# A feed-forward block split by batch element, one half in the tail of the attention before it, one beside the first group of the attention after it, and a fixed VectorE order for the first tokens

## The chip, the cores and the metric

The kernel runs as one program on one core of a Trainium2 chip. A time is the device time of one execution in microseconds (us). The engines are TensorE (PE, matmuls and transposes; PEld is its weight load), VectorE (DVE), ScalarE (ACT), GpSimd (POOL) and the DMA queue of SyncE (SP). All arithmetic is in 32-bit floats.

## What is computed

A batch of B = 2 sequences of 512 tokens of width 512 goes through eight residual blocks. The change touches the first three:

```
x = x + attn_latent(layernorm(x))   # 32 heads, 12-wide query latents, 4-wide key latents
x = x + ffn_lora(layernorm(x))      # y = x @ W.T + bias, plus per batch element a low-rank
                                    # adapter x @ A.T @ B.T, chosen by lora_start_indices
x = x + attn_gqa(layernorm(x))      # 32 query heads in 8 groups of 4, causal, rotary
...                                 # ffn_lora, attn_mla, ffn_moe, attn_mha, ffn_moe
layernorm(x) = (x - mean) / sqrt(var + 1e-5)
```

## The kernel before

x stays in on-chip memory as eight tiles of 128 tokens (x0 to x3 are batch element 0, x4 to x7 are 1). A layer norm of a tile is `centred` (L170: statistics on VectorE, a power on GpSimd in `inv_sqrt`, then xn on VectorE, in one of two "xn" buffers) and `place` (L184: four transposes on PE, one copy on ScalarE into xT of the batch element). Products against x read xT. PSUM has eight banks, handed out in turn (`turn`, L145); before `hold` (L150) each turn takes a tile from a pool, after it one of eight fixed tiles.

Most engines' instruction order is chosen by the framework's scheduler, which may move an instruction ahead of others when it is ready by its own reckoning. Inside `tc.manual_schedule(engines={...})` the named engines keep the order of the program. An instruction on an engine's queue waits in order: what stands behind a waiting one waits too.

**First attention** (`attn_latent_small`, L399). `prepare(b)` makes the layer norms of four tiles, key latents, query latents, the queries of all heads and the values. `prepare(0)` runs first, in the scheduler's order; the eleven pieces of `prepare(1)`, `fold` and `fold_bias` are handed to `run_quartets` as `extra`. There are 16 quartets u (batch element, half, index) of four heads. For a quartet: `score` (16 matmuls with 32 rows each, for the maxima, each reduced on VectorE), `maxima`, `transposed` (16 matmuls with 32 rows, each followed by an exponential on ScalarE into a probabilities tile of one of three kinds), `values`. In step u of the loop (L343) the scores of u+1 alternate with the transposed scores of u; then come values(u) and maxima(u+1). Pieces `divide`, `flatten`, `project` and `norms` of the quartet before lie between; after quartet 7 and 15 they finish a batch element: divide by the sums, flatten on GpSimd, project on PE and add to x. `norms` (L629) makes the feed-forward block's layer norms of x0 to x3 during quartets 8 to 10. PE keeps the program's order here. In the last two steps only transposed scores and values of quartet 15 are left, then its divide, flatten and project.

**Feed-forward block** (`ffn_lora`, L665). Loads the weight (1 MB, buffer kind "w8", five buffers) and the adapter, scales the adapter by `k.coef` (from `adapter_coefficients`, L644), and makes one adapted weight for each batch element: eight 48-row matmul pairs, each added to the weight on VectorE. Then, for each of eight tiles, a `chain` of four matmul steps (eight instructions in the trace), the sum into x, and a layer norm: beside batch 0's products those of x4 to x7 for this block, beside batch 1's products those of x0 to x3 for the next attention (`back=True`, a permuted token order).

**Second attention** (`attn_gqa`, L707). Loads wdk, rotary tables, the first group's weights; `latents(0, m)` are four chains on xT of batch 0. A group of four heads m then goes through query products (`queries`, three parts per pair of heads; sums of weights on GpSimd, additions and rotation on VectorE and GpSimd), `softmax` per head, and `beside(m, j)`, which places the work of neighbouring groups after head j: prepare_keys(m+1) at j = 2, prepare_values(m+1) at j = 3, values(m-1), output(m-1, ...). For m = 0 there is no earlier group. PE keeps the program's order here too.

Of the kernel before, what the change touches and what calls it, by code (L numbers as in the profile page):

```python
# [45 lines left out]
class Block:  # L46


    def __init__(self, ctx, tc, x, out):
        nc = self.nc = tc.nc  # L50
        self.tc = tc
        self.out = out
        pool = lambda name, bufs, **kw: ctx.enter_context(tc.tile_pool(name=name, bufs=bufs, **kw))
        self.const = pool("const", 1)
        self.w = pool("w", 2)
        self.work = pool("work", 2)
        self.small = pool("small", 6)
# [19 lines left out]
        self.warm()  # L77
# [5 lines left out]
    def warm(self):  # L83


        ps = self.tr()
        for i in range(56):
            self.nc.tensor.transpose(ps[:, bass.ts(i % 4, P)], self.ident, self.ident)

    def load_x(self, b):  # L90
# [76 lines left out]
        return last.ins  # L167


    def centred(self, t, bias=None):  # L170

        nc = self.nc
        stats = self.sm(6, "ln_stats")
        nc.vector.bn_stats(stats, self.x[t])
        mv = self.sm(2, "ln_mv")
        nc.vector.bn_aggr(mv, stats)
        rstd = self.inv_sqrt(mv[:, 1:2], 1.0, 1e-5)
        xn = self.work.tile([P, D], F32, tag="xn", name="xn")
        nc.vector.tensor_scalar(xn, self.x[t], mv[:, 0:1], rstd, ALU.subtract, ALU.mult)
        if bias is not None:  # L180
            self.add_bias(t, bias)
        return xn
# [27 lines left out]
        self.nc.gpsimd.tensor_tensor(self.x[t], self.x[t], bias, ALU.add)  # L210

    def add_to_x(self, t, ps):
        self.nc.vector.tensor_tensor(self.x[t], ps, self.x[t], ALU.add)

# [119 lines left out]
                )  # L334

    @staticmethod
    def run_quartets(n, score, maxima, transposed, values, after, extra=()):

        due, extra = [], list(extra)
        for u in range(-1, n + 1):  # L343
            pieces = [due.pop(0)] if due else []
            for j in range(NT):
                for m, (kind, g) in enumerate(
                    ((0, 0), (1, 1), (0, 2), (1, 3), (0, 1), (1, 0), (0, 3), (1, 2))
                    if j
                    else ((0, 0), (0, 1), (0, 2), (0, 3), (1, 0), (1, 1), (1, 2), (1, 3))
                ):  # L350
                    if kind == 0 and u + 1 < n:
                        score(u + 1, j, g)
                    if kind == 1 and 0 <= u < n:
                        transposed(u, j, g)
                if extra and u >= 0:
                    extra.pop(0)()
                elif pieces and j < 3:
                    of, done = pieces[0]
                    if done < len(after):
                        after[done](of)  # L360
                        pieces[0] = (of, done + 1)
            for of, done in pieces:
                for f in after[done:]:
                    f(of)
            if 0 <= u < n:
                values(u)
                due.append((u, 0))
            if u + 1 < n:
                maxima(u + 1)

    @staticmethod
    def run_ordered(n, lead, order, score, maxima, transposed, values, after):
# [26 lines left out]
def attn_latent_small(k, a):  # L399
# [7 lines left out]
    nc, tc = k.nc, k.tc  # L407
    with ExitStack() as ctx:
# [19 lines left out]
        for i in range(2):  # L428
            m = one([P, NT, P], f"nm{i}")
# [7 lines left out]
        for vk in vals:  # L437
            nc.gpsimd.memset(vk, 0.0)
        halves = one([P, 8], "halves")
        nc.vector.tensor_scalar(halves, bqk, 0.5, None, ALU.mult)  # L440

        def prepare(b):

# [28 lines left out]
            def values():  # L472

                tp = k.turn()
                for t in range(NT):
                    nc.tensor.transpose(tp[:, bass.ts(t, P)], keys[b][:, bass.ts(t, P)], k.ident)
                part = tp.rearrange("p (t d) -> p t d", t=NT)[:, :, 0:5]
                for i in range(4):
                    nc.vector.tensor_copy(vals[b][:, :, i, 5 * i : 5 * i + 5], part)

            norms = [lambda t=t: k.layernorm(b * NT + t, k.turn) for t in range(NT)]
            return norms + [latents, queries, lambda: heads(0), lambda: heads(1), values]

        def fold():

# [22 lines left out]
                k.add_bias(t, bias)  # L508

        folded = one([P, D], "folded")  # L510
        for piece in prepare(0):
            piece()
        k.masks()
        adapter_coefficients(k, a)
        extra = prepare(1) + [fold, fold_bias]

        quartets = [(b, half, i) for b in range(B) for half in range(2) for i in range(4)]
        qm, probs, sums, ctxs = {}, {}, {}, {}
# [26 lines left out]
        def transposed(u, kc, g):  # L545
            b, half, i = quartets[u]
            if (u, kc) not in probs:
                n = (4 * u + kc) % 3
                if n == 0:
                    probs[u, kc] = k.other()  # L550
                else:
                    pool, tag, bufs = ((lp, "pT", 2), (k.w, "w8", 5))[n - 1]
                    probs[u, kc] = pool.tile([P, 4, S], F32, tag=tag, name="pt", bufs=bufs)
# [75 lines left out]
        def norms(u):  # L629

            i = u - len(quartets) // 2 + 1
            if i in (1, 2):
                for t in (2 * i - 2, 2 * i - 1):
                    k.place(t, normal.pop(t), k.turn)
            if i in (0, 1):
                for t in (2 * i, 2 * i + 1):
                    normal[t] = k.centred(t)

        after = [divide, flatten, project, norms]
        with tc.manual_schedule(engines={mybir.EngineType.PE}):  # L640
            k.run_quartets(len(quartets), score, maxima, transposed, values, after, extra)


def adapter_coefficients(k, a):  # L644
# [17 lines left out]
    nc.vector.tensor_reduce(k.coef, r, AX.X, ALU.add)  # L662


def ffn_lora(k, a):  # L665

    nc, tc = k.nc, k.tc  # L670
    R = 48
    with ExitStack() as ctx:
        lp = ctx.enter_context(tc.tile_pool(name="f0", bufs=2))
        w = k.load(a["f0_w"], [P, KC, D], "w8", 5)

        la = k.load(a["f0_a"], [P, D], "w3", 6)
        lb = k.load(a["f0_b"], [P, D], "w3", 6)
        bias = k.load_row(a["f0_bias"], D, "bias")
        nc.vector.tensor_scalar(la, la, k.coef, None, ALU.mult)

        adapted = [k.w.tile([P, KC, D], F32, tag="w8", name="adapted", bufs=5) for b in range(B)]
        for m in range(KC):
            out = [k.turn() for b in range(B)]
            for b in range(B):
                own = slice(64 * b, 64 * b + R)
                nc.tensor.matmul(
                    out[b], la[own, bass.ts(m, P)], lb[own], start=True, stop=True
                )
            for b in range(B):
                nc.vector.tensor_tensor(adapted[b][:, m], out[b], w[:, m], ALU.add)  # L690

        for t in range(NT):
            k.add_bias(t, bias)
        for b in range(B):
            for t in range(NT):
                ps = k.turn()
                k.chain(
                    ps, [(k.xT[b][:, c, bass.ts(t, P)], adapted[b][:, c]) for c in range(KC)]
                )
                k.add_to_x(b * NT + t, ps)  # L700
                if b == 0:
                    k.layernorm(NT + t, k.turn, bias=bias)
                else:
                    k.layernorm(t, k.turn, back=True)


def attn_gqa(k, a, bound):  # L707

# [8 lines left out]
    with ExitStack() as ctx:  # L717
# [188 lines left out]
        def beside(m, j):  # L906


            before = m - 1 if 0 < m <= len(groups) else None

            normal(m, j, 5, 1, True)
# [877 lines left out]
```

## Time and profile before

| | |
|---|---|
| Three runs | 2122.04, 2124.99, 2126.02 us; median 2124.99 |
| The profiled execution | 2125.91 us, of which its span is 2124.2 us |
| Busy share of PE, DVE, ACT, POOL | 96%, 64%, 35%, 46% |
| Mean granted TensorE clock | 0.982 of full |
| First scores on PE | 29.45 us |
| Last scores of the first attention end | 277.2 us |
| First chain of the feed-forward block | 306.1 us |
| First latents of the second attention | 338.86 us |
| First exponents of its group 0 | 369.43 us |

The profile is one execution of the program, with every engine's instructions in time. In the rows that the prediction shows, "sc<-qm,keys" means that tile sc was written from qm and keys; "x8" counts instructions; a bracket gives the idle time just before on that engine and what ended it. L164 is `chain`, L190 and L195 the transposes and the copy of `place`, L524 the score matmul, L555 and L558 the transposed score and its exponential, L566 the values, L588 to L624 divide, flatten and project, L686 and L690 the adapter matmul and its addition, L829 to L874 the queries and their rotation, L237 the second attention's scores, L309 its values. Matmuls overlap in the pipeline, so a row's duration is longer than its spacing to the next.

### The profile page before, as it was taken

To read this page: it belongs to the slowest core of one execution; us is meant where nothing else is said; L and a number is where in the kernel's file an instruction comes from. 1 tells how busy PE (TensorE), PEld (TensorE's weight loads), DVE (VectorE), ACT (ScalarE), POOL (GpSimd) and SP (SyncE) were. 2 spreads that over 40 slices of the span, in tenths; PEclk is the share of its full clock that TensorE was granted. 3 is DMA by queue.
4 is the path that set the end of the run, shared out by engine and by line. 5 is a ranking of instruction groups with operands and counts; after the bars stand their busy time and mean duration, and the time that the engine had idled before them with its cause. 6 is when DMAs were issued, how large, how long until landed. Compare 5 with 4: busy or idle time off the path is not lost. (4 is left out here: it accounts for less than half of the span.)

```text
span 2124.2 us, 40108 instructions
## 1 busy us (share of the span) xinstructions
PE 2046.3 (96%) x15556; PEld 1154.9 (54%) x15556; DVE 1349.7 (64%) x3575; ACT 744.9 (35%) x2072; POOL 967.1 (46%) x1239
## 2 busy tenths in 40 slices
PE   8999999899999999999999988999999989999998
PEld 5444435666666666666666444545454444554654
DVE  6578754765675566666765547666666684855845
ACT  2465631222222222222322135454445311441531
POOL 1101013767565467666763246555555556115220
PEclk8999999999999999999999989999999999999999
DMA  3000022222222222222221321010101003002001
GB/s 99 16 1 1 21 90 76 83 71 70 90 73 72 82 73 80 71 90 71 73 71 36 115 60 50 25 50 25 50 22 50 3 6 68 3 2 40 2 2 40
DMA packets 70220, 107.43 MB, mean 51 GB/s; under 512 B 13698, under 2 KB 50690, under 8 KB 63236
## 3 DMA queue, kind: packets, MB, share of 16 engines
q1 hardware_dynamic: 69380, 103.71, 15.7%
q8 instruction: 126, 2.06, 0.4%
q10 hardware_dynamic: 640, 1.05, 0.3%
q14 instruction: 74, 0.61, 0.1%
HBM read 80.61 MB, written 2.10 MB: 39 GB/s over the span
## 5 line engine op out<-in xcount | busy, mean ns | idle before, releaser
L258 ACT ACTIVATE room<-room,nmax 128x128 f32<-128x128 f32 (+3 forms) x384 | 212.1, 554 | 475.6 <-DVE nmax L248 474.4
L269 POOL TENSOR_SCALAR room<-room,invs 128x128 f32<-128x128 f32 (+3 forms) x384 | 197.8, 536 | 138.6 <-DVE invs L266 138.6
L309 PE MATMUL sc<-turned,vals 32*128 32x128 f32 (+7 forms) x1090 | 188.2, 421 | 0.0
L309 PE MATMUL tp<-turned,vals 32*128 32x384 f32 (+7 forms) x720 | 163.8, 410 | 2.5 <-DVE q L838 1.9
L237 PE MATMUL sc<-kT,q 128*32 128x256 f32 (+3 forms) x1496 | 135.4, 397 | 11.4 <-DVE invs L266 7.9
L282 DVE STREAM_TRANSPOSE turned<-room 128x1152 f32<-128x1152 f32 x80 | 109.0, 1363 | 41.2 <-POOL room L269 38.7
L309 PEld LDWEIGHTS sc<-turned,vals 32*128 32x128 f32 (+1 forms) x1090 | 121.8, 170 | 9.2 <-issue 3.3
L309 PE MATMUL pj<-turned,vals 32*128 32x256 f32 (+7 forms) x602 | 124.8, 421 | 1.3 <-DVE turned L282 1.3
L205 POOL TENSOR_TENSOR rstd<-ve,mhalf 128x1 f32<-128x1 f32 x80 | 44.5, 560 | 166.7 <-DVE ve L203 142.6
L873 POOL TENSOR_TENSOR q<-q,cosq 128x512 f32<-128x512 f32 x60 | 89.4, 1491 | 60.6 <-DVE t L870 60.6
L237 PE MATMUL tp<-kT,q 128*32 128x32 f32 (+15 forms) x1072 | 98.5, 401 | 11.1 <-DVE invs L266 7.3
L309 PEld LDWEIGHTS tp<-turned,vals 32*128 32x128 f32 (+1 forms) x720 | 96.6, 168 | 15.6 <-issue 8.3
L237 PE MATMUL pj<-kT,q 128*32 128x96 f32 (+15 forms) x1048 | 100.0, 415 | 1.7 <-DVE invs L266 0.9
L164 PE MATMUL sc<-w,room 128*128 128x512 f32 (+1 forms) x224 | 100.1, 593 | 0.0
L309 PE MATMUL av<-turned,vals 32*128 32x384 f32 (+7 forms) x372 | 99.9, 419 | 0.0
L269 POOL TENSOR_SCALAR probs<-probs,invs 128x128 f32<-128x128 f32 (+3 forms) x128 | 65.8, 534 | 64.4 <-DVE invs L266 60.5
L164 PE MATMUL sc<-w,ctxT 128*128 128x512 f32 x208 | 94.1, 595 | 0.0
L258 ACT ACTIVATE probs<-probs,nmax 128x128 f32<-128x128 f32 (+3 forms) x128 | 71.1, 556 | 65.3 <-DVE nmax L248 64.0
L874 POOL TENSOR_TENSOR q<-q,t 128x512 f32<-128x512 f32 x64 | 88.3, 1380 | 7.2 <-DVE q L873 3.2
L1135 POOL TENSOR_TENSOR t<-t,sinq 128x512 f32<-128x512 f32 x32 | 40.9, 1278 | 110.9 <-DVE invs L266 102.3
L281 DVE STREAM_TRANSPOSE turned<-room 128x128 f32<-128x128 f32 x80 | 24.4, 305 | 99.4 <-POOL room L269 99.3
L555 PE MATMUL sc<-qm,keys 32*128 32x512 f32 x198 | 85.5, 637 | 0.0
(610 smaller groups left out, 6284.0 us busy)
## 6 DMA issues: line engine op xcount, KB each, us to landing
w<-in_b_wq SPq DMA_DIRECT2D x16, 1024.0 KB, 5.0
w<-in_b_wo SPq DMA_DIRECT2D x16, 1024.0 KB, 5.7
vals<-v SPq DMA_DIRECT2D x256, 64.0 KB, 2.0
w<-in_m_wo SPq DMA_DIRECT2D x8, 1024.0 KB, 5.8
w<-in_b_wk SPq DMA_DIRECT2D x16, 256.0 KB, 2.6
w<-in_b_wupv SPq DMA_DIRECT2D x16, 256.0 KB, 2.6
w<-in_f_w SPq DMA_DIRECT2D x4, 1024.0 KB, 6.0
w<-in_m_wqn SPq DMA_DIRECT2D x8, 384.0 KB, 3.0
```

The source lines that it names most:

```text
L164: last = self.nc.tensor.matmul(out, lhsT, rhs, start=(i == 0), stop=(i == len(pairs) - 1))
L205: self.nc.gpsimd.tensor_tensor(r, ve, self.mhalf, ALU.pow)
L237: nc.tensor.matmul(ps[32 * i : 32 * i + 32, a - lo : b - lo], q[:, at : at + 32], keys[:, a:b], start=True, stop=True,)
L258: nc.scalar.activation(row, row, AF.Exp, bias=nmax, scale=-1.0, accum_out=total[:, qt : qt + 1])
L269: self.nc.gpsimd.tensor_scalar(row, row, inv[:, qt : qt + 1], 1.0, ALU.mult, ALU.mult)
L281: self.nc.vector.transpose(out[:, self.WIDE - P :], probs[:, last : last + P])
L282: self.nc.vector.transpose(out[:, :last], probs[:, :last])
L309: self.nc.tensor.matmul(out[:, :, :n], values(i, j), rhs, start=(j == blocks[0]), stop=(j == stop[i]),)
L555: nc.tensor.matmul(ps, keys[b][rows[g], bass.ts(kc, P)], qm[u][rows[g]], start=True, stop=True)
L873: mul.tensor_tensor(q, q, tables["cosq"], ALU.mult)
L874: nc.gpsimd.tensor_tensor(q, q, t2, ALU.add)
L1135: nc.gpsimd.tensor_tensor(t2, t2, sinq, ALU.mult)
```

## The change

- **Start.** `centred` is split into `statistics` and the rest. For the first four tiles and for `prepare(0)` both PE and VectorE keep the program's order: warm transposes (30 at first, then 5 or 10 after each placement, where 56 stood at the beginning), statistics of two tiles, their xn, their placement. The layer norms of x4 to x7 and the other extra pieces may be put no earlier on VectorE than behind the last placement's xn (`issue_after(first)`), the adapter coefficients no earlier than behind the last copy of `prepare(0)`. `halves` moves behind the query latents.
- **Banks.** `k.hold()` comes first, so all turns of the first attention use the eight fixed banks.
- **Block.** `ffn_lora`'s parts become a class. It is made in `norms` after quartet 7, and its bias is added to x0 to x3 there. From quartet 9 on, one kind of probabilities tile lies in the query tile of batch 0 and not in "w8" buffers.
- **Tail.** The loop of `run_quartets` ends a step earlier. Quartet 15's transposed scores follow its maxima directly; values(14) come after the sixth of them, and adapter matmuls after every second one from the tenth on. Then the block's products of x0 to x3 alternate with values(15), divide, flatten and project; the layer norms of x0 to x3 for the second attention follow.
- **Second attention.** The layer norms of x4 to x7 come between its four latents, and the products of x4 to x7 first thing in beside(0, j), j = 0 to 3.

The second use of `ffn_lora`, after the second attention, keeps its order.

```diff
+    def statistics(self, t):
...
+        return mv, self.inv_sqrt(mv[:, 1:2], 1.0, 1e-5)
...
-    def run_quartets(n, score, maxima, transposed, values, after, extra=()):
+    def run_quartets(n, score, maxima, transposed, values, after, extra, ending):
...
-        for u in range(-1, n + 1):
+        for u in range(-1, n - 1):
...
-            if 0 <= u < n:
+            if 0 <= u < n - 2:
                 values(u)
                 due.append((u, 0))
-            if u + 1 < n:
-                maxima(u + 1)
+            maxima(u + 1)
+        for i in range(NT * 4):
+            transposed(n - 1, i // 4, i % 4)
+            if i == 5:
+                values(n - 2)
+                for f in after:
+                    f(n - 2)
+            if i > 5 and i % 2:
+                ending.pop(0)()
+        ending.pop(0)()
+        values(n - 1)
+        for f in ending:
+            f()
...
-        for piece in prepare(0):
-            piece()
+        with tc.manual_schedule(engines={mybir.EngineType.PE, mybir.EngineType.DVE}):
+            k.warm(30)
+            for t in range(0, NT, 2):
+                known = [k.statistics(t + i) for i in range(2)]
+                rows = [k.centred(t + i, known=known[i]) for i in range(2)]
+                for i in range(2):
+                    k.place(t + i, rows[i], k.turn)
+                    k.warm(5 + 5 * i)
+            first = k.latest
+            latents, queries, *rest = prepare(0)
+            latents()
+            queries()
+            nc.vector.tensor_scalar(halves, bqk, 0.5, None, ALU.mult)
+            for piece in rest:
+                piece()
         k.masks()
-        adapter_coefficients(k, a)
-        extra = prepare(1) + [fold, fold_bias]
+        def behind(piece):
+            def f():
+                with tc.issue_after(first):
+                    piece()
+            return f
+        with tc.issue_after(k.latest):
+            adapter_coefficients(k, a)
+        extra = [behind(f) for f in prepare(1) + [fold, fold_bias]]
...
+                elif n == 2 and u > len(quartets) // 2:
+                    at = 4 * (((4 * u + kc) // 3) % 2)
+                    probs[u, kc] = qs[0][:, at : at + 4]
...
+            if i == 0:
+                with tc.issue_after(k.latest):
+                    blocks.append(AdaptedBlock(k, a))
...
-                    normal[t] = k.centred(t)
+                    normal[t] = k.centred(t, blocks[0].bias)
+        adapt = [lambda m=m: blocks[0].adapt(m) for m in range(KC)]
+        feed = [lambda t=t: blocks[0].product(0, t) for t in range(NT)]
+        tokens = [lambda t=t: k.layernorm(t, k.turn, back=True) for t in range(NT)]
+        ending = [lambda: None] + adapt + feed[:2]
+        ending += [lambda: divide(last), feed[2], lambda: flatten(last), feed[3]]
+        ending += [lambda: project(last)] + tokens
...
+class AdaptedBlock:
+    R = 48
+    def __init__(self, k, a):
+        self.w = k.load(a["f0_w"], [P, KC, D], "w8", 5)
+        self.la = k.load(a["f0_a"], [P, D], "w3", 6)
+        self.lb = k.load(a["f0_b"], [P, D], "w3", 6)
+        self.bias = k.load_row(a["f0_bias"], D, "bias")
+        k.nc.vector.tensor_scalar(self.la, self.la, k.coef, None, ALU.mult)
+        self.adapted = [
+            k.w.tile([P, KC, D], F32, tag="w8", name="adapted", bufs=5) for b in range(B)
+        ]
+    def adapt(self, m):
...
+    def product(self, b, t):
+        k = self.k
+        ps = k.turn()
+        k.chain(ps, [(k.xT[b][:, c, bass.ts(t, P)], self.adapted[b][:, c]) for c in range(KC)])
+        k.add_to_x(b * NT + t, ps)
...
         def beside(m, j):
+            if m == 0:
+                block.product(1, j)
...
             for m in range(KC):
                 latents(0, m)
+                k.layernorm(NT + m, k.turn, bias=block.bias)
...
     k = Block(ctx, tc, a["x"], out)
-    attn_latent_small(k, a)
+    k.hold()
+    block = attn_latent_small(k, a)
     bound = CausalBound(k, a)
-    k.hold()
-    ffn_lora(k, a)
-    attn_gqa(k, a, bound)
+    attn_gqa(k, a, bound, block)
     ffn_lora(k, a)
```

More of the change, by code (lines that the diff above doesn't have):

```diff
@@ L76, in __init__ @@
         make_identity(nc, self.ident)
-        self.warm()
         self.mhalf = self.const.tile([P, 1], F32, tag="mhalf", name="mhalf")
@@ L81, in __init__, with warm @@
         nc.gpsimd.memset(self.ones, 1.0)
-    def warm(self):
-        ps = self.tr()
-        for i in range(56):
+    def warm(self, n):
+        ps = self.turn()
+        for i in range(n):
             self.nc.tensor.transpose(ps[:, bass.ts(i % 4, P)], self.ident, self.ident)
@@ L167, in chain @@
         return last.ins
-    def centred(self, t, bias=None):
+    def statistics(self, t):
         nc = self.nc
@@ L176, in centred @@
         nc.vector.bn_aggr(mv, stats)
-        rstd = self.inv_sqrt(mv[:, 1:2], 1.0, 1e-5)
+        return mv, self.inv_sqrt(mv[:, 1:2], 1.0, 1e-5)
+    def centred(self, t, bias=None, known=None):
+        nc = self.nc
+        mv, rstd = known or self.statistics(t)
         xn = self.work.tile([P, D], F32, tag="xn", name="xn")
-        nc.vector.tensor_scalar(xn, self.x[t], mv[:, 0:1], rstd, ALU.subtract, ALU.mult)
+        self.latest = nc.vector.tensor_scalar(
+            xn, self.x[t], mv[:, 0:1], rstd, ALU.subtract, ALU.mult
+        ).ins
         if bias is not None:
@@ L212, in add_to_x @@
     def add_to_x(self, t, ps):
-        self.nc.vector.tensor_tensor(self.x[t], ps, self.x[t], ALU.add)
+        self.latest = self.nc.vector.tensor_tensor(self.x[t], ps, self.x[t], ALU.add).ins
     ORDER = (3, 1, 0, 2)
@@ L439, in attn_latent_small @@
         halves = one([P, 8], "halves")
-        nc.vector.tensor_scalar(halves, bqk, 0.5, None, ALU.mult)
         def prepare(b):
@@ L478, in values @@
                 for i in range(4):
-                    nc.vector.tensor_copy(vals[b][:, :, i, 5 * i : 5 * i + 5], part)
+                    to = vals[b][:, :, i, 5 * i : 5 * i + 5]
+                    k.latest = nc.vector.tensor_copy(to, part).ins
             norms = [lambda t=t: k.layernorm(b * NT + t, k.turn) for t in range(NT)]
-            return norms + [latents, queries, lambda: heads(0), lambda: heads(1), values]
+            return (norms if b else []) + [latents, queries, lambda: heads(0), lambda: heads(1), values]
         def fold():
@@ L636, in norms @@
                 for t in (2 * i, 2 * i + 1):
-                    normal[t] = k.centred(t)
+                    normal[t] = k.centred(t, blocks[0].bias)
+        blocks = []
+        last = len(quartets) - 1
+        adapt = [lambda m=m: blocks[0].adapt(m) for m in range(KC)]
[4 more added lines that the diff above has]
+        ending += [lambda: project(last)] + tokens
         after = [divide, flatten, project, norms]
         with tc.manual_schedule(engines={mybir.EngineType.PE}):
-            k.run_quartets(len(quartets), score, maxima, transposed, values, after, extra)
+            k.run_quartets(
+                len(quartets), score, maxima, transposed, values, after, extra, ending
+            )
+        return blocks[0]
 def adapter_coefficients(k, a):
@@ L662, in adapter_coefficients @@
     nc.vector.tensor_reduce(k.coef, r, AX.X, ALU.add)
-def ffn_lora(k, a):
[L670 to L690, printed above, removed]
-        for t in range(NT):
[L693 to L704, printed above, removed]
@@ L707, in attn_gqa @@
-def attn_gqa(k, a, bound):
+class AdaptedBlock:
+    R = 48
+    def __init__(self, k, a):
+        self.k = k
+        self.w = k.load(a["f0_w"], [P, KC, D], "w8", 5)
[7 more added lines that the diff above has]
+    def adapt(self, m):
+        k, nc = self.k, self.k.nc
+        out = [k.turn() for b in range(B)]
+        for b in range(B):
+            own = slice(64 * b, 64 * b + self.R)
+            nc.tensor.matmul(
+                out[b], self.la[own, bass.ts(m, P)], self.lb[own], start=True, stop=True
+            )
+        for b in range(B):
+            nc.vector.tensor_tensor(self.adapted[b][:, m], out[b], self.w[:, m], ALU.add)
+    def product(self, b, t):
[3 more added lines that the diff above has]
+        k.add_to_x(b * NT + t, ps)
@@ L715, in attn_gqa @@
+def ffn_lora(k, a):
+    block = AdaptedBlock(k, a)
+    for m in range(KC):
+        block.adapt(m)
+    for t in range(NT):
+        k.add_bias(t, block.bias)
+    for b in range(B):
+        for t in range(NT):
+            block.product(b, t)
+            if b == 0:
+                k.layernorm(NT + t, k.turn, bias=block.bias)
+            else:
+                k.layernorm(t, k.turn, back=True)
+def attn_gqa(k, a, bound, block):
     nc, tc = k.nc, k.tc
```

## The prediction

> **What bounds the kernel now.** I read the page first: TensorE (PE) is busy 96% of a span of 2124.2 us, so the stages matter in which it is not, or in which it is busy below its rate. The change touches the first 30 us and the stretch from 277 to 426 us, so I asked for these stages (columns: stretch and length; busy us of PE, weight loads, VectorE, ScalarE, GpSimd, with instruction counts; granted TensorE clock; DMA share; GB/s).
>
> ```profile
> 0.00:11.80 11.80, 8.88 (x56) 8.65 (x56) 6.27 (x20) 1.28 (x1) 6.53 (x20) 1.00 0.73 240
> 11.80:17.10 5.30, 3.08 (x16) 2.40 (x16) 3.05 (x11) 2.25 (x4) 2.05 (x4) 0.71 0.92 254
> 17.10:29.40 12.30, 11.43 (x36) 4.82 (x36) 5.11 (x14) 1.30 (x3) 0.00 (x0) 0.85 0.26 85
> 29.40:41.00 11.60, 8.78 (x38) 4.79 (x36) 11.37 (x23) 1.12 (x2) 0.00 (x0) 0.87 0.00 0
> ```
>
> PE idles and its clock falls before the first scores (29.45); from 29.4 to 41 VectorE is the limit (11.37 of 11.60). Second, the end of the first attention, the feed-forward block and the start of the second attention:
>
> ```profile
> 277.20:282.20 5.00, 4.21 (x38) 1.34 (x36) 2.55 (x5) 0.72 (x2) 0.00 (x0) 1.00 0.01 3
> 282.20:292.60 10.40, 10.27 (x64) 4.12 (x64) 0.05 (x1) 7.95 (x16) 0.00 (x0) 1.00 0.00 1
> 292.60:302.50 9.90, 6.65 (x18) 2.88 (x18) 4.39 (x7) 0.59 (x1) 0.61 (x1) 0.83 0.00 0
> 306.10:338.90 32.80, 31.58 (x99) 15.27 (x97) 22.18 (x51) 4.70 (x8) 17.69 (x24) 1.00 0.44 159
> 384.00:405.60 21.60, 20.31 (x156) 13.13 (x148) 16.17 (x38) 4.85 (x17) 14.68 (x19) 0.87 0.09 25
> ```
>
> The block itself (306.1 to 338.9) is limited by PE at full clock: nothing is to be saved there. What can be saved lies around it: from 282.2 the last quartet's 16 exponentials are paced by ScalarE (one per 0.48 us, 7.95 us), from 292.6 a chain of divide, flatten, project leaves PE idle 3.3 us and then slow. Third, the waits of PE from 366 to 430:
>
> ```profile
> PE tp L237 <- POOL q L874: 3.9, 1, 3.9
> PE sc L237 <- POOL q L874: 2.8, 2, 1.5
> PE tp L309 <- DVE q L838: 1.9, 1, 1.9
> ```
>
> Fourth, the timeline, for the order at the start and for the prices:
>
> ```profile
> 3.46 0.69 DVE L174 BATCH_NORM_STATS2 ln_stats<-x 128x6 f32<-128x512 f32 x1 [3.46 <-DMA x<-in_x]
> 11.23 0.99 DVE L179 TENSOR_SCALAR xn<-x,ln_mv,rstd 128x512 f32<-128x512 f32 x2
> 17.13 5.53 PE L164 MATMUL tp<-room,w 128*128 128x512 f32 x8 [0.68 <-ACT room L195]
> 303.87 0.68 DVE L690 TENSOR_TENSOR adapted<-sc,w 128x512 f32<-128x512 f32 x1
> 314.78 3.60 PE L164 MATMUL av<-adapted,room 128*128 128x512 f32 x8
> 318.22 0.60 PE L190 MATMUL sc<-ident,xn 128*128 128x128 f32 x4
> ```
>
> The first token tile is on chip at 3.46 but normalised only at 11.23: statistics of later tiles stand ahead of it on VectorE.
>
> **The start.** Now statistics of tiles 0 and 1, then their normalisation, then 2 and 3. One tile's statistics are 0.69 + 0.18 + 0.14 us with gaps, about 1.1; the power on GpSimd 0.55; the normalisation 0.5. From 3.46: tiles 0, 1 done at 6.8, tiles 2, 3 at 10.2 (tile 2 landed at 6.2). PE: of the 56 warm transposes, 10 and 11 start in the first two stretches of 2 us, then 15, then 21; so 30 end near 7.2. Then four placements of 0.43 with 5, 10, 5 and 10 more transposes (0.107 each, 3.2 us): 12.1, and ScalarE's last copy ends by then. The latents start at 12.3 instead of 17.13: -4.8. Their eight matmuls took 5.53 us at a low clock against 3.60 in a chain at full clock: -1.9 if the clock holds.
>
> Here a rule speaks against the change. The Trainium skill, "TensorE: Matmul & The Clock Gate", section "Part 4: PE-mode transpose", says transposes don't count as busy for the clock gate, so warming with them should leave the latents at half rate: the 1.9 would be lost, and the queries' chain (3.60) would also double, +3.6. The rows say otherwise: the warm transposes themselves quicken from 10 to 21 per 2 us, and the clock fell only in the stretch with gaps. I follow the rows; by the rule this part is worth about 5.5 less.
>
> Against it: the adapter coefficients (seven small VectorE instructions, 0.17 + 0.22 + 0.15 + 0.16 + 0.15 + 0.16 + 0.16 = 1.2 us) ran in idle time at 17.8; now they follow the value copies, into the stretch that VectorE bounds: +1.2. Statistics of tiles 4 to 7 (about 1 us each) may fill VectorE's gap from 10 to 20 as before, or land in the bound stretch: 0 to +2, taken as +0.5, since the scheduler put them early before. Sum -6.7 + 1.7 = **-5.0** (ends -7 and 0).
>
> **The tail.** Before, from the end of the last scores (277.2) to the latents of the second attention (338.86): 61.7 us. After, in PE's written order:
> - maxima of the last quartet come ahead of the values of the one before; the reductions end at 278.46, transposes 0.66, addition 0.68, gaps: first exponents' matmul at 280.2, 3.0 us;
> - 16 transposed scores, now in pairs on two of the four row groups: 8 x 0.86 = 6.9 (ScalarE needs 7.7 for the exponentials, hidden under the values and adapter matmuls between);
> - values of two quartets, 2 x 3.5 = 7.0;
> - adapter matmuls, 4 x 0.86 = 3.5 (3.6 before, 302.5 to 306.1); their eight additions of 0.68 lie on an idle VectorE;
> - four products of batch 0, 4 x 3.43 = 13.7 (314.78 to the transposes at 318.22);
> - about 11 changes between 32-row, 64-row and full matmuls, 0.10 each (the 0.53 from 352.26 to 352.79 against 0.43): 1.1;
> - two sets of transposes 0.9, the wait for ScalarE's copy of the context 0.9, project 8 x 0.43 = 3.4 (5.3 before, at the low clock), four layer norms' transposes 1.8, and 1.5 for two norm buffers and the last copy.
>
> Together 43.7: the latents start at 320.9, **-18.0**. The divide and flatten (0.56, 0.42 and 0.61 us) lie under products 2 and 3. The change of array shape is the second rule: "TensorEngine Tiling (Array Packing)", "Key Properties", says a change of mode drains TensorE, which speaks against interleaving. At the row's 0.10 it is the 1.1; if each drain showed a full 32-row matmul's 0.59, +5.4. I take the row. If the hidden exponentials are not hidden, at most 2 us return. Ends -20 and -13.
>
> Layer norms of batch 1 move between the latents: 4 x 0.45 = **+1.8**; their bias additions (1.27) and powers (0.55) on GpSimd, with the eight weight sums (0.73 to 0.9), are 13 us in 17.
>
> **The second half of the block**, four products (13.7 us) in group 0, each ahead of what beside() issues next. Products 0 and 1 come before and after the exponents of head 1, ahead of PE's wait of 3.9. The chain that this wait is for starts after product 0, so it moves by 3.43, plus 0.7 for one addition in VectorE's queue, which is full from 376 to 386: head 2's exponents move by 4.1, not 6.9. Then the 6.7 us from 383.7 ran at a clock of 0.57; at full clock they take 3.8, so +1.2 stands. Products 2 and 3: +6.9, less the later wait of 1.3: +6.8. The 1.9 at 417 and the half clock behind it (2.9 us at 0.50) come from VectorE's backlog; I let half of these 3.3 go: **+5.2** (ends +2 and +13.7).
>
> DMA: the adapted weights keep a "w8" buffer until product 3, so the second output weight (issued at 337.8) comes after it; it is needed two groups later and costs nothing. Probabilities in the old query tile: two places, as the other kinds have; nothing.
>
> Sum -5.0 - 18.0 + 1.8 + 5.2 = -16.0 against the profiled execution's 2125.9 (span 2124.2 and 1.7 around it): 2109.9. The median of the three runs, 2125.0, is 0.9 lower: **2109**.
>
> **Rivals.**
> - *The second half is paid in full.* VectorE and GpSimd bound group 0 (15.3 of 18.0 us busy from 366 to 384) and their chains move with the products: -5.0 - 18.0 + 1.8 + 13.7 = -7.5, 2117.5. Against it: PE is the one that waits, and product 1 stands behind the chain's start.
> - *The latents wait for their weight.* In the trace the load of wdk is issued at 304.04, behind rope tables that wait for the attention's memory. If that order stays, it is issued 1 us after project's end and needs 5 to 6 us, with three tables of 256 KB ahead: latents 5 us late, 2114. Against it: its buffer is now free long before.
> - *More is hidden*: group 0 at +2 and the start at -7: -21, 2104.
> - *Slower: the PSUM banks held from the first instruction.* If the fixed banks make each quartet of the first attention wait, 16 quartets pay. From 1 us per quartet the gain is gone; from 1.3 (20.3 us = 16.0 + 4.25) it is slower beyond the bound. Against it: the order and distance of the turns are the same eight, and the second attention already runs on held banks with PE busy 30.00 of 30.00 us from 430 to 460.
>
> **How the numbers follow.** Likeliest case 0.55; paid in full 0.15 (a fifth of it with a poor start, within 0.2%); weight late 0.12; more hidden 0.12; held banks 0.06. A measurement of this kernel tells 0.2%, 4.25 us, from no change. Faster 0.55 + 0.12 + 0.12 + 0.09 = 0.88, same 0.06, slower 0.06. Range: from 2101, the gains' ends, to 2120, past the full price and the late weight.
>
> **What would show it.** Right: latents of the start by 13 us and first scores near 24; from the last scores to the second attention's latents 44 us, clock 1.00 throughout; the wait of 3.9 under 1.5. Wrong: a DMA wait at the latents; the start's clock still near 0.7; quartets of more than 16.0 us (239.9 us from the first maxima at 40.8 to the last at 280.75, over 15); new waits of PE on VectorE between products in the tail.

## The result, and the profile after

The changed kernel takes 2104.84 us (median of 4 runs, 2103.46 to 2109.19) against 2123.7 (4 runs, 2122.04 to 2126.02): ratio 0.9914, 95% interval 0.9896 to 0.9932, so 0.9% faster. 2109 was forecast, with 2101 to 2120 around it. A second set of five runs of it, in the experiments, gave 2108.11 against 2121.99 (ratio 0.9927): the gain is 18.9 us in the first set and 13.9 in the second, and 16.0 was forecast. The profiled execution took 2103.46 us, span 2101.4 (before 2124.2).

The stages after, in the columns of the stages before. The start:

```profile
0.00:12.10 12.10, 10.18 (x67) 10.18 (x68) 7.43 (x20) 3.04 (x4) 6.53 (x19) 1.00 0.76 240
12.10:23.40 11.30, 10.46 (x47) 4.99 (x45) 6.03 (x17) 1.86 (x4) 2.77 (x4) 1.00 0.62 206
23.40:36.00 12.60, 10.13 (x42) 4.96 (x40) 12.03 (x30) 1.15 (x2) 0.00 (x0) 0.83 0.00 1
```

In the second stage PE is busy for 10.46 of 11.30 us; before, it was busy for 3.08 of 5.30. The clock column reads 1.00 where a trace has no clock record yet, so its first stage has to be read from the transposes:

```profile
1.92 6.31 PE L86 MATMUL pj<-ident 128*128 128x128 f32 x30 [1.92 <-POOL ident masks.py:199]
12.00 1.26 PE L86 MATMUL pj<-ident 128*128 128x128 f32 x10
```

The first 30 start 0.21 us apart, the last ten 0.11. The trace has the change at 7.74 us, between one start and the next; from there to the first scores the clock is whole. The third stage is VectorE's, as before, and the clock falls there as before. The tail and group 0:

```profile
272.10:276.20 4.10, 2.44 (x18) 1.24 (x16) 1.97 (x4) 1.18 (x3) 0.00 (x0) 1.00 0.01 4
276.20:288.60 12.40, 12.40 (x70) 3.35 (x68) 4.55 (x7) 7.80 (x16) 0.00 (x0) 1.00 0.00 1
288.60:306.70 18.10, 18.10 (x71) 7.43 (x70) 8.77 (x19) 0.13 (x1) 2.22 (x4) 1.00 0.25 88
306.70:315.10 8.40, 6.44 (x29) 3.53 (x27) 7.65 (x15) 2.84 (x5) 3.80 (x6) 1.00 0.60 213
344.00:366.00 22.00, 20.54 (x146) 13.01 (x149) 19.10 (x39) 5.38 (x16) 15.19 (x17) 1.00 0.37 108
366.00:388.00 22.00, 22.00 (x146) 12.91 (x139) 18.59 (x45) 5.45 (x19) 14.24 (x20) 1.00 0.16 53
```

From 276 to 307 PE has no gap: the exponentials (7.80 us of ScalarE) and the chain of divide and flatten lie under the values, the adapter matmuls and four products. From 366 to 388 it is busy for 22.00 of 22.00 us at full clock; this is the part of group 0 in which it waited 3.9 us before and then ran slowly (the prediction's row from 384.00, clock 0.87). The scores at which it waited, before and after:

```profile
383.77 0.44 PE L237 MATMUL tp<-kT,q 128*32 128x32 f32 x6 [3.89 <-POOL q L874]
364.97 0.32 PE L242 MATMUL tp<-kT,q 128*32 128x32 f32 x5
```

After, nothing is waited for. The longest four waits of PE from 255 to 420 (columns: us in total, times, longest):

```profile
PE tp L314 <- DMA vals<-v: 2.1, 1, 2.1
PE av L242 <- POOL q L944: 1.5, 1, 1.5
PE sc L598 <- DVE qm L581: 0.9, 1, 0.9
PE av L579 <- DVE nm L571: 0.8, 1, 0.8
```

The waits of 3.9 and 1.3 are gone. The first line names a DMA, but PE's next instruction started at 401.70, just after VectorE's addition that frees a bank, and VectorE had itself waited for GpSimd:

```profile
401.22 0.42 DVE L908 TENSOR_TENSOR q<-tp,q 128x256 f32<-128x256 f32 x1 [2.46 <-POOL q L925]
```

It is the 1.9 us of before; in the second profile of the same kernel the same wait of 2.1 us is put down to VectorE. The way from the first tile to the latents:

```profile
3.49 0.70 DVE L172 BATCH_NORM_STATS2 ln_stats<-x 128x6 f32<-128x512 f32 x1 [3.49 <-DMA x<-in_x]
5.52 0.54 DVE L182 TENSOR_SCALAR xn<-x,ln_mv,rstd 128x512 f32<-128x512 f32 x1
13.10 3.60 PE L162 MATMUL tp<-room,w 128*128 128x512 f32 x8
```

The first normalisation is at 5.52 instead of 11.23, and the eight latent matmuls take 3.60 instead of 5.53.

Landmarks on PE in each profile (start times, us; "forecast" is the time before plus the prediction's sums; for the first scores its text says "near 24"):

| | before | after | forecast | after, second profile |
|---|---|---|---|---|
| First scores | 29.45 | 23.49 | 22.8 | 22.79 |
| Maxima of the second quartet | 58.38 | 53.28 | 53.4 | 52.44 |
| Last scores' last matmul | 276.66 | 271.58 | 271.7 | 270.70 |
| Second attention's latents | 338.86 | 315.11 | 315.9 | 314.25 |
| Its first keys | 352.79 | 331.08 | 331.6 | 330.21 |
| Last matmul of its first values | 426.01 | 409.23 | 410.0 | 410.06 |
| First folded keys of the third attention | 1240.76 | 1223.99 | 1224.8 | 1224.82 |
| Span | 2124.2 | 2101.4 | 2108.2 | 2106.0 |

Up to the first values the gain is 16.8 us, in the second profile 15.9, and 800 us later, at the third attention, it still is. The other 6.0 us of the first two spans' difference come behind that, where nothing was changed. One line each, before and after, for the stretch that begins there; in the same 22 us the second has 117 matmuls and the first 81:

```profile
1240.00:1262.00 22.00, 20.30 (x81) 9.79 (x85) 6.72 (x38) 7.07 (x30) 7.49 (x12) 0.61 0.18 38
```

```profile
1222.00:1244.00 22.00, 18.06 (x117) 9.01 (x115) 9.82 (x54) 9.96 (x38) 7.96 (x12) 0.92 0.16 38
```

The granted clock was 0.61 and 0.92. An experiment below (VectorE left free), whose code differs from the changed kernel's only in VectorE's order in the start, has it low again:

```profile
1230.00:1252.00 22.00, 20.21 (x81) 9.86 (x85) 6.61 (x38) 6.96 (x30) 7.40 (x11) 0.61 0.17 38
```

The rest of the run from that landmark on, which is the same in every kernel here, takes 874.8 to 883.4 us in the 13 profiles: 883.4 in these two with the low clock, 877.4 and 881.2 in the two of the changed kernel. So these microseconds come from the clock, and the change does not remove them. What decides on them is taken up in the last section. This is why the experiments are read by landmarks first and by ratios second.

### The profile page after: what moved, and what is told of

Its sections match the earlier page's. It is cut to its first block, busy times and chain, and to the rows that moved or that the text cites. A ratio compares the mean times of both kernels' runs of the same rounds, so it can differ in the third digit from the quotient of the medians.

```text
span 2101.4 us, 40138 instructions
## 1 busy us (share of the span) xinstructions
PE 2031.9 (97%) x15560; PEld 1147.1 (55%) x15560; DVE 1351.0 (64%) x3575; ACT 745.4 (35%) x2072; POOL 970.4 (46%) x1239
## 5 line engine op out<-in xcount | busy, mean ns | idle before, releaser
L314 PE MATMUL pj<-turned,vals 32*128 32x384 f32 (+7 forms) x708 | 184.9, 422 | 0.0
L314 PE MATMUL tp<-turned,vals 32*128 32x256 f32 (+7 forms) x770 | 147.1, 420 | 2.5 <-DMA vals<-v 2.1
L242 PE MATMUL sc<-kT,q 128*32 128x256 f32 (+4 forms) x1528 | 134.0, 384 | 6.8 <-DVE invs L271 4.1
L162 PE MATMUL sc<-w,room 128*128 128x512 f32 (+1 forms) x256 | 112.1, 582 | 0.0
L314 PEld LDWEIGHTS pj<-turned,vals 32*128 32x128 f32 (+1 forms) x708 | 104.0, 169 | 4.0 <-issue 1.6
L162 PE MATMUL sc<-w,ctxT 128*128 128x512 f32 x224 | 101.5, 596 | 0.0
L218 DVE TENSOR_TENSOR x<-sc,x 128x512 f32<-128x512 f32 x79 | 54.2, 686 | 73.0 <-PE sc L162 70.3
L242 PE MATMUL tp<-kT,q 128*32 128x512 f32 (+4 forms) x984 | 91.7, 407 | 4.5 <-DVE invs L271 3.8
L253 DVE CUSTOM_DVE_ANT_0 room<-sc,mask 128x256 f32<-128x256 f32 (+3 forms) x149 | 70.7, 474 | 35.6 <-PE sc L242 34.1
L242 PE MATMUL pj<-kT,q 128*32 128x288 f32 (+3 forms) x968 | 89.6, 404 | 2.9 <-POOL q L1211 1.9
```

What stands on the lines that cost most here:

```text
L162: last = self.nc.tensor.matmul(out, lhsT, rhs, start=(i == 0), stop=(i == len(pairs) - 1))
L218: self.latest = self.nc.vector.tensor_tensor(self.x[t], ps, self.x[t], ALU.add).ins
L242: nc.tensor.matmul(ps[32 * i : 32 * i + 32, a - lo : b - lo], q[:, at : at + 32], keys[:, a:b], start=True, stop=True,)
L253: nc.vector.tensor_tensor_reduce(out=row, in0=ps[:, :kv], in1=self.mask_back[:, :kv] if qt % 2 else self.mask[:, S - kv :], op0=ALU.add, o ...
L314: self.nc.tensor.matmul(out[:, :, :n], values(i, j), rhs, start=(j == blocks[0]), stop=(j == stop[i]),)
```

## The experiments

Theory: the gain is 5 us at the start and 18 in the tail, less 1.8 and 5.2 for what moves behind it. Rivals: fixed banks cost time, group 0 hides nothing, the tail gains by its own order.

**The start alone.** The kernel before with the changed start (the diff's hunks from `warm` to `extra`, no `hold`).

> The kernel before with the new start alone (warm transposes spread, VectorE's order fixed, adapter coefficients behind the value copies), banks and everything later as before. If the start is worth what the traces show, first scores come near 23.5 us (29.45 before), the last scores of the first attention end near 272.1 (277.2), and the rest of the time line keeps its lengths: 61.7 us from there to the second attention's latents; the whole is 5 us faster, about 2118.5. Rival: the start's gain needs the fixed banks or is given back in the first quartets; then the last scores end at 275 or later and the whole is within 2 us of before.

Measured: first scores 22.77, last scores 271.23, 62.2 us from there to the latents (62.2 before); ratio 0.9976 (0.9964 to 0.9988), 5.1 us. The start is a part of its own: it brings what was forecast, and the rest of the time line keeps it.

**Banks from the pools in the first attention.**

```diff
-    k.hold()
     block = attn_latent_small(k, a)
     bound = CausalBound(k, a)
+    k.hold()
```

> The changed kernel with the eight fixed banks taken only after the first attention, as before. If fixed banks cost nothing, all landmarks stay: first scores 23.5, last scores' end 272.1, latents 315.1, whole within 2 us of the changed kernel. Rival, that fixed banks make quartets wait: a quartet (15.9 us from maxima to maxima) becomes shorter by up to 1 us and the last scores end up to 16 us earlier.

Measured: first to last scores 247.9 us against 248.1 and 247.9 in the two profiles of the changed kernel; latents at 314.35; ratio 0.9929 (0.9912 to 0.9945). Fixed banks cost nothing: this rival is out.

**The second half in front of the second attention.**

```diff
                 k.layernorm(NT + m, k.turn, bias=block.bias)
+            for t in range(NT):
+                block.product(1, t)
...
-            if m == 0:
-                block.product(1, j)
```

> The changed kernel with the four products of batch 1 in front of the second attention's keys and not beside group 0; the same work. If group 0 hides most of them, the stretch from the second attention's latents to the end of its first values (315.1 to 409.5, 94.4 us in the changed kernel) grows by 13.7 - 4.9 = 8.8 us and PE's waits of 3.9 and 1.3 us in group 0 come back, with a half clock behind the long one; whole 8 to 9 us slower than the changed kernel. Rival, that the second half is paid in full wherever it stands: the stretch grows by less than 2 us.

Measured: latents to the end of the first values 103.5 us (94.1 and 95.8 in the changed kernel), ratio 0.9963 (0.9953 to 0.9973). PE's waits from 345 to 425:

```profile
PE av L242 <- POOL q L944: 3.9, 1, 3.9
PE tp L314 <- DVE q L908: 1.9, 1, 1.9
PE sc L242 <- POOL q L944: 1.5, 1, 1.5
PE tp L242 <- POOL q L944: 1.3, 1, 1.3
```

The waits of before are back to the tenth. Beside group 0 the four products cost 13.7 us less 7.7 to 9.4; the whole, 2114.15 us, is 7.5 above the 2106.6 of the version before it. "Paid in full" is out.

**The first half behind project.**

```diff
-        ending = [lambda: None] + adapt + feed[:2]
-        ending += [lambda: divide(last), feed[2], lambda: flatten(last), feed[3]]
-        ending += [lambda: project(last)] + tokens
+        ending = [lambda: None] + adapt + [lambda: None]
+        ending += [lambda: divide(last), lambda: flatten(last)]
+        ending += [lambda: project(last)] + feed + tokens
```

> The changed kernel with the four products of batch 0 behind the first attention's project and not between its last steps; the same work. If they fill the chain of divide, flatten and project, the stretch from the last scores' end to the latents (43.0 us) grows by the 3.3 us that PE idled there before, about 1 us for the last values that now wait for exponentials, and 1.9 for project at half clock (5.3 against 3.4): 5 to 6 us. Rival, that the gain of the tail comes from the last quartet's own order (values moved, adapter matmuls between): it grows by less than 2 us.

Measured: 52.0 us from the last scores to the latents, 8.4 more than the 43.5; ratio 0.9954 (0.9937 to 0.9971). Waits of PE in the tail, the three that are new:

```profile
PE av L195 <- DVE ve L208: 2.5, 1, 2.5
PE sc L662 <- POOL flat L652: 1.9, 1, 1.9
PE tp L631 <- DVE raw L621: 0.9, 1, 0.9
```

2.8 us are the chain's waits, and the clock was half for 3.4 us at 298.8, during project: both as expected. 2.5 more come from a layer norm that now follows its product at once, and another half clock of 3.4 us at 275.0 (about 1.7 us) is one that other runs show too. The direction holds; the size was under-estimated by these two.

**No warm transposes.** `k.warm(30)` and `k.warm(5 + 5 * i)` taken out.

> The changed kernel without any warm transposes. If transposes release TensorE's clock (as the trace before shows, 10 in the first 2 us, 21 in the fourth), the latents start up to 1.2 us earlier (no ten transposes ahead of them) but at half clock, their eight matmuls take 5 to 7 us and not 3.6, and the first scores come 1 to 3 us later than the 22.8 to 23.5 of the changed kernel. Rival, that transposes don't count for the clock: the latents' rate is what it was and the first scores come at the same time or 1.2 us earlier.

Measured: first scores at 25.00, 1.5 to 2.2 later. The latents start between the 12.39 and 13.10 of the two profiles of the changed kernel, and take longer than 3.60:

```profile
12.59 5.61 PE L162 MATMUL tp<-room,w 128*128 128x512 f32 x8 [0.68 <-ACT room L200]
```

The trace has the clock's release at 16.48 us; in the twelve profiles with warm transposes it comes at 4.85 to 7.74, when PE has run nothing but transposes. So the warm transposes do release the clock. The whole, ratio 0.9929 (0.9912 to 0.9947), can't show 2 us.

**VectorE left free in the start.** `manual_schedule` there for PE alone.

> The changed kernel with PE's order kept in the start but VectorE's left to the scheduler, the later tiles still held behind the fourth tile's normalisation. The first normalisation then stands behind four statistics. If what mattered was that tiles 4 to 7 were moved out of the way, the first placement is 2 us later, the fourth at most 0.5 us, and the first scores are within 0.5 us. Rival, that the pairwise order itself brings the gain: the first scores come 3 us or more later.

Measured: first scores at 25.09, 1.6 to 2.3 later, neither the 0.5 nor the 3. The four statistics ahead cost little; another instruction did:

```profile
11.40 0.17 DVE L540 TENSOR_SCALAR halves<-a_bqk 128x8 f32<-128x8 f32 x1 [2.65 <-DMA a_bqk<-in_a_bqk]
```

The scheduler put `halves`, which needs a 4 KB load, ahead of the third and fourth normalisation, and they stood behind it for 2.65 us. By this trace the fixed order pays by where `halves` stands; no run moved `halves` alone. The ratio, 0.996 (0.9942 to 0.9977), holds the long half clock shown above as well.

**Late coefficients.**

```diff
-        with tc.issue_after(k.latest):
-            adapter_coefficients(k, a)
         extra = [behind(f) for f in prepare(1) + [fold, fold_bias]]
+        def coefficients():
+            with tc.issue_after(k.latest):
+                adapter_coefficients(k, a)
+        extra.append(coefficients)
```

> The changed kernel with the adapter coefficients behind the values of batch 1 (in the third quartet step) and not behind those of batch 0. If their seven small instructions cost what was put on VectorE's bound stretch, the first quartet's maxima come 1.0 to 1.2 us earlier after the first scores (12.0 us in the changed kernel), and everything later too; whole 1 us faster. Rival: they lie in gaps of VectorE; no change.

Measured: first scores to the last maxima matmul of the first quartet 11.38 us instead of 12.03: 0.65, half of what was expected; seven small instructions of 1.2 us in sum overlap with the reductions beside them. The last scores come 1.3 earlier after the first, but the whole was not faster, ratio 0.9938 (0.9921 to 0.9954): in its profile the tail took 46.9 us and not 43.5. The tail's clock, in the last column but two:

```profile
272.00:276.00 4.00, 3.20 (x12) 1.33 (x12) 0.66 (x1) 1.20 (x3) 0.00 (x0) 0.61 0.01 4
276.00:280.00 4.00, 4.00 (x22) 0.91 (x24) 0.00 (x0) 1.85 (x4) 0.00 (x0) 0.54 0.00 0
```

**Warm transposes between the first scores.** The kernel with late coefficients, and in `score`:

```diff
+            if u == 0:
+                k.warm(3)
             ps = k.turn()
```

> As the kernel with late coefficients, and three more warm transposes ahead of each of the first quartet's 16 score matmuls, where VectorE bounds and PE has idle time. If the half clock of 10.2 us that follows the first scores comes from PE's idle time there, it disappears, the stretch from the first to the second quartet's maxima (17.6 to 17.8 us) becomes about 16, and the whole is 1.5 to 2 us faster than with the late coefficients alone. Rival: the transposes delay the scores or the clock drops all the same; no gain, or up to 5 us lost (48 transposes of 0.107 to 0.2 us).

Measured: ratio 1.0063 (1.004 to 1.0087), 26 us slower than with late coefficients alone. Neither the gain came nor the loss of up to 5 us that the rival allowed.

```profile
36.00:54.00 18.00, 18.00 (x35) 6.57 (x34) 4.84 (x7) 0.00 (x0) 0.00 (x0) 0.50 0.00 0
```

Two things went wrong. Full transposes between them keep the 32-row score matmuls from running side by side: one score with its transposes takes 1.5 us at full clock, and VectorE needs 0.6. And PE, busy without a gap by the profile's count, was given half the clock, for these 18 us and for 41.0 in all, from 26.9 on.

**The changed kernel again, and two versions.** Run side by side. First the changed kernel:

> The changed kernel once more, beside the two versions below. Its profile had no half clock at all between 42 and 1229 us, while five experiments with the same tail had one of 3.4 or 6.8 us at 273 to 276 us. If that clock is chance and not the kernel, this run shows 3.4 to 6.8 us at half clock there, 1.7 to 3.4 us more from the last scores to the latents (43.5 in the first profile), and a span 2 to 5 us above the 2101.4 of the first. Rival: a kernel's clock repeats; the span and the stretch are as in the first profile.

Measured: 2108.11 us, ratio 0.9927 (0.9912 to 0.9942); tail 43.55 us without a half clock, so not as expected for this run. Nine profiles have the changed kernel's tail, at least up to the last quartet's transposed scores. Six of them fell to half clock there and three did not, and among both kinds are kernels whose last scores start within 0.1 us of each other:

```profile
275.30:278.70 3.40, 3.40 (x31) 0.94 (x32) 0.00 (x0) 2.63 (x6) 0.00 (x0) 1.00 0.00 0
```

```profile
275.30:278.70 3.40, 3.40 (x18) 0.79 (x20) 0.00 (x0) 2.61 (x6) 0.00 (x0) 0.50 0.00 0
```

The first is this run, the second the one with the second half in front. Where the tail is otherwise the same, the half clock costs 1.6 to 3.7 us. So it does not repeat with the kernel; but it follows a pattern. In each of the 13 traces the clock changes only at whole steps of 3.413 us behind its first release. How far into such a step the last score matmul starts, as a fraction of the step, parts the profiles:

| Profiles | Place in the step | Half clock, us |
|---|---|---|
| Changed kernel, banks from the pools, changed kernel again | 0.30, 0.49, 0.48 | none |
| Second half in front, first half behind project, VectorE free | 0.64, 0.75, 0.84 | 3.4, 3.4, 6.8 |
| No warm transposes, late coefficients, transposes between scores | 0.03, 0.08, 0.14 | 6.8 each |

No run set this place on purpose, so it is an order that fits all nine and not an experiment.

The first version takes late coefficients and puts three adapter steps where PE waits:

```diff
+            if u == n - 2:
+                ending.pop(0)()
+                ending.pop(0)()
             maxima(u + 1)
+        ending.pop(0)()
...
-        ending = [lambda: None] + adapt + feed[:2]
+        idle = [lambda: None] * 2
+        ending = adapt[:3] + idle + adapt[3:] + idle + feed[:2]
```

> Late coefficients, and two of the four adapter steps ahead of the last quartet's maxima, a third behind them, where PE waits 0.8 and 0.9 us and then runs lone 32-row matmuls. If the half clock at 273 us comes from these waits, it is gone in this kernel, the stretch from the last scores to the latents is 42 to 43 us in every run, and the whole is 1.3 us (coefficients) and 1 to 4 us (tail) faster than the changed kernel run beside it. Rival: the clock falls for the 32-row matmuls and not for the waits, or the exponentials are now exposed; no gain beyond the 1.3.

Measured: tail 41.3 us, no half clock there in its profile; 2103.17 us, ratio 0.9907 (0.9893 to 0.9922), 4.9 us under the changed kernel beside it. The two intervals overlap a little; the five runs, 2100.78 to 2105.15, lie below the changed kernel's 2105.00 to 2109.78 but for 0.15 us.

```profile
270.20:274.60 4.40, 4.17 (x21) 1.41 (x16) 4.40 (x9) 1.27 (x3) 0.00 (x0) 1.00 0.00 0
```

PE is busy 4.17 of 4.40 us around the maxima. Its last score matmul starts at 0.67 of a step, and that of the next version, which has the same tail and no half clock there either, at 0.79: between 0.64 and 0.84 all three profiles of the unchanged tail fell. That speaks for the waits as the cause, in two profiles. The second version also moves the last product:

```diff
-            if m == 0:
-                block.product(1, j)
+            if (m, j) in ((0, 0), (0, 1), (0, 2), (1, 1)):
+                block.product(1, j if m == 0 else 3)
```

> As the version before, and the fourth product of batch 1 not in group 0 but ahead of the first values, where PE waits 2.1 us for a bank that VectorE frees only after GpSimd's additions, and where the clock halves. If the product covers that wait, the stretch from the latents to the end of the first values (94 to 97 us) is 2 to 4 us shorter. Rival: the chain behind the wait moves with the product, and the waits of group 1's first exponents come back; within 1 us.

Measured: latents to the end of the first values 94.3 us, 1.5 under the changed kernel beside it (half clock for 3.4 us at 402.2) and 2.8 under the first version (half clock for 6.8 us at 397.6). It has no half clock there itself, like the first profile of the changed kernel, which took 94.1. The waits of PE from 255 to 420, the first two:

```profile
PE pj L242 <- POOL q L953: 2.7, 1, 2.7
PE av L242 <- POOL q L953: 1.5, 1, 1.5
```

The wait of 2.1 is covered and another of 2.7 has come back: the rival's mechanism. Between profiles without a half clock nothing is gained. 2101.47 us, ratio 0.9904 (0.9889 to 0.9919): it beats the kernel before, and its interval lies beside the changed kernel's 0.9912 to 0.9942 with a small overlap. It is not told apart from the first version.

## Why the prediction was right

- **Start, -5.0.** -5.1 and -5.9 at the second quartet's maxima, -5.1 by the ratio of the start alone. The latents were forecast at 12.3 and started at 13.10 and 12.39; the 0.7 between the two is when the clock was released, so that the 30 transposes ended at 8.07 or 7.34. The forecast of 7.2 for their end misread a row: 10, 11, 15 and 21 count a transpose that crosses an edge in both stretches, and the thirtieth in fact starts at 7.70 before. Against the rule on transposes that the prediction cites, its reading of the rows was right: transposes alone released the clock, and without them the latents took 5.61. The coefficients were priced at 1.2 and cost 0.65; the statistics of tiles 4 to 7, put at 0.5, lay in VectorE's gap from 10.7 to 14.1 and cost nothing there. What was not seen is `halves`: by its trace, most of what the fixed VectorE order itself brings.
- **Tail, -18.0.** -18.7: 43.0 us from the end of the last scores, where the listed sum gave 43.7. Of the 18.7, 15.5 are the four products and the four placements of batch 1 that moved away (13.7 and 1.8); they cost 6.9 us where they went in the first profile (2.0 and 4.9) and 8.6 in the second. The tail itself gained 3.2 us. The price of changing the array's shape, 0.10, was enough; the rule that a change drains the array did not show as more. "Clock 1.00 throughout" holds in both profiles of the kernel but was luck: six of nine such tails fell to half clock. That term was missing.
- **Layer norms between the latents, +1.8.** 2.0.
- **Group 0, +5.2.** From the latents to the end of the first values it took 87.2 us before, 94.1 and 95.8 after; less 2.0 for the layer norms that is +4.9 and +6.6. The total is right by terms that offset each other. Head 2's exponents were to move by 4.1 and moved by 2.9: the wait of 3.9 disappeared whole (forecast under 1.5), and the half clock behind it too. Half of the 3.3 us at the first values was to go; the wait stayed (2.1 for 1.9), since its cause is GpSimd's queue and not VectorE's backlog, and the half clock behind it is in the second profile and not in the first.
- **Rivals.** Paid in full: refuted (103.5 against 94.1 us). Weight late: wdk was issued at 184.81, far ahead. Banks: refuted. More hidden: the first set's total lies between the likeliest case and this one, but not by its reason; the first two spans' extra 6.0 us are the clock later on. (In the chances, a fifth of 0.15 is 0.03; "same" holds 0.06.)

## What to carry to other kernels

A block that PE bounds at full rate still gains when it is cut up and laid into the waits of its neighbours. The price is read from those waits: here a piece ahead of a wait whose chain started before it was free (the second product: head 2's exponents moved by 0.5 less than head 1's), and a piece ahead of the chain's start was paid (the first product: 3.4), or, in the last experiment, brought another wait back. The order fixed by hand paid here because the scheduler had put an instruction with a late load ahead of the critical one.

## What the runs showed of the hardware

The clock can be halved while PE has no gap in the profile, which models the ends of matmuls: 18.00 of 18.00 us busy at 0.50, with short transposes and single 32-row matmuls. The runs don't tell which of the two counts too little.

A half clock in the middle of the run depends on where the work falls in the steps of 3.413 us in which the clock changes, and the first release, at 4.85 to 7.74 us, sets these steps anew in each execution. For the tail the table above shows it. At the third attention the first folded keys lie at 0.40 and 0.37 of a step in the two profiles that then have 17.1 us of half clock (from 1242.8 and 1232.7), at 0.32 in the one that has 3.4 us, and at 0.89 to 1.19 in the other ten, which have none there. So the same instructions in the same order are halved or not: of the spans' difference of 22.8 us, up to 6 are this.
